# Performer features in a hybrid network: pairs of heads in 32 rows of the array, four chunks of tokens per call

## The chip, the core and the metric

The kernel runs on one core of a Trainium2 chip. A core has a matrix engine (TensorE, "PE" in the profile, with "PEld" for its weight loads), a vector engine (VectorE, "DVE"), a scalar engine for activation functions (ScalarE, "ACT"), a general engine (GpSimd, "POOL"), and a queue for transfers (SyncE, "SP"). They run side by side and wait for each other by semaphores. TensorE reads its operands from the on-chip memory (SBUF) and writes to a second one (PSUM), which has 8 banks of 512 f32 columns on 128 partitions. The metric is device time in microseconds (us), from one launch, as the median of several runs.

## What is computed

The network takes `x` of shape (8, 128, 16, 16), in f32: 8 images of 256 tokens with 128 features. It runs an adder convolution, a Mamba block, an attention with a mixture of experts, a Performer with eight layers, and a spectral layer. The change is in the Performer's attention. Its reference, cut to that:

```python
B, W, D, H, DEP, LAT = (8, 8192, 128, 8, 4, 10)   # H = 8 heads
DH = D // H                                       # 16
M = 44                                            # random features of a head

def softmax_kernel(data, proj, is_query, eps=0.0001):
    dn = data.shape[-1] ** (-0.25)
    ratio = proj.shape[0] ** (-0.5)
    dd = jnp.einsum('bhnd,md->bhnm', data * dn, proj)
    diag = jnp.sum(data * data, axis=-1, keepdims=True) * 0.5 * (dn * dn)
    if is_query:
        mx = jnp.max(dd, axis=-1, keepdims=True)
    else:
        mx = jnp.max(dd, axis=(-1, -2), keepdims=True)
    return ratio * (jnp.exp(dd - diag - mx) + eps)

def attn(t, i):
    q = (t @ Wq[i] + bq[i]).reshape(Bb, N, H, DH).transpose(0, 2, 1, 3)
    ...
    q = apply_rotary(q, sin, cos)
    k = apply_rotary(k, sin, cos)
    qp = softmax_kernel(q, proj[i], True)
    kp = softmax_kernel(k, proj[i], False)
    d_inv = 1.0 / jnp.einsum('bhnm,bhm->bhn', qp, jnp.sum(kp, axis=2))
    ctx = jnp.einsum('bhnm,bhnd->bhmd', kp, v)
    o = jnp.einsum('bhnm,bhmd->bhnd', qp, ctx) * d_inv[..., None]
    ...
    return o @ Wo[i] + bo[i]

for i in range(lo, lo + DEP):
    t = t + attn(layer_norm(t, ln1_g[i], ln1_b[i]), i)
    u = layer_norm(t, ln2_g[i], ln2_b[i])
    t = t + (jax.nn.gelu(u @ W1[i] + b1[i], approximate=False) @ W2[i] + b2[i])
```

`dd` are the features: each head's 16 values of a token against 44 random vectors. The same 44 vectors serve all heads.

## The kernel before

**Tokens and streams.** The activations lie as [128 features, 2048 tokens]. They are cut into 4 blocks of 512 tokens (`BLK`), two images each. In the Performer two *streams* (`_performer_stream`, line 1327) run two blocks each. Each stream has its own pools: `two` and `many` in SBUF, and `psum` with four banks (line 1227), so that the two streams share the eight banks evenly. `bank(S, shape, name)` (line 1263) takes the next of a stream's four banks in turn, and waits until the tile that held it four allocations ago is done with.

**Who goes when.** The streams are Python generators. `interleave` (line 1257) steps both in turn, from yield to yield, and that order of tracing is the order of priority for the scheduler. The scheduler then sorts the instructions of each engine by readiness. Stream 0 starts 16 steps (`HALF_LAYER`) before stream 1. Inside a layer the two blocks of a stream are stepped in turn too (line 1351). A layer of a stream is: a layer norm (`_norms`, 3 steps), the attention of both blocks (`_performer_attention`, line 1402), a second layer norm, the first MLP matmuls with GELU (`p1`, `g3`, lines 1360 to 1365, 4 steps), and the second MLP matmuls (`p2`, line 1370, 2 steps). In the profile both MLP matmuls are called `p`: `p<-u,lw` is the first, `p<-g,lw` the second.

**ACT's tables.** `Tables.use` (line 277) preloads a table of activation functions and orders ACT's instructions around it: everything traced before it comes before it. GELU has its own table. If an Exp or Ln of the other stream stands in a GELU stretch, the build inserts loads around it; in the profile these are ACT_TABLE_LOAD rows.

**The attention of one block,** in the order of its code:

- `rotated` (line 1412): keys and queries by one matmul each (`pa`), bias and rotary angles on DVE (`ro`, `rk`, `rq`), the sum of both parts on POOL (line 1426). Squares for `diag` go through ACT and a matmul (`sq`, `pl`, `dg`).
- *Features of the keys* (lines 1459 to 1471): for each of four chunks of 128 tokens one matmul, `pf` [128 tokens, 8 heads x 44]. The stationary operand is the chunk of `k`, 128 rows (the features of all heads) by 128 tokens. The moving operand `w["f"]` [128, 352] is block-diagonal: the 16 rows of a head hold the 44 vectors in that head's 44 columns, zeros elsewhere. DVE takes the maximum of each head (`mxk`) and subtracts it (`ek`); ACT takes the exponential.
- The maximum over all tokens (lines 1474 to 1486; `m2`, `pm`, `gm`, `dm`, `pg`), the factors that it leaves, and the values `pv`, `vo`.
- *Features of the queries*, function `query(c)`: the same as for keys for chunk `c`, with the maximum of each token and head and its `diag`. Two chunks are done here (lines 1524 to 1527).
- *The context* (lines 1531 to 1556): `pc`, keys' features times values; for each pair of heads and each chunk one matmul with `ek` as stationary operand [128, 88] and 34 moving columns. Then `ks` and `ctx`.
- `turned(c, ex)`: four transposes `px`, one for each pair of heads (88 rows), and one ACT copy to `qp` [88, pair, 512 tokens] (line 1522). The loop of lines 1558 to 1562 turns chunk `c` and computes query chunk `c + 2`.
- `pn` (lines 1565 to 1574): queries' features times context, with 32 output columns for each pair of heads, so that four pairs lie in four groups of columns of the array; then the division (`rd`), the output matmul `po`, and the sum into `H`.

All matmuls are f32. Line 265 is the helper `mm`; most matmuls stand under it and are told apart by their tiles.

Of the kernel before, what the change touches and what calls it, by code (L numbers as in the profile page):

```python
# [10 lines left out]
F32 = mybir.dt.float32  # L11
AF = mybir.ActivationFunctionType
ALU = mybir.AluOpType
AX = mybir.AxisListType
PSUM = bass.MemoryType.PSUM

P = 128
# [3 lines left out]
BLK = 512  # L21
# [14 lines left out]
NH = 8  # L36
DH = 16
M = 44
HM = NH * M
PAIR = 2 * M  # L40
NPAIR = NH // 2
PD = 2 * DH
# [252 lines left out]
def bc(ap, axis, n):  # L295

    a = ap.unsqueeze(axis)
    shape = list(a.shape)
    shape[axis] = n
    return a.to_broadcast(shape)  # L300
# [561 lines left out]
class _Fuse:  # L862
# [23 lines left out]
    def bank(self, shape, name):  # L886
        return self.psum.tile(shape, F32, tag="f", name=name)
# [439 lines left out]
def _performer_stream(S, blocks):  # L1327
# [18 lines left out]
    for i in range(NL):  # L1346
        w = _layer(S, i)
        sums = [two.tile([P, 2], F32, tag=f"us{j}", name="us3") for j in range(2)]
        us = yield from _norms(S, h, S.v(f"ln1_g{i}"), S.v(f"ln1_b{i}"), sums)
        parts = [_performer_attention(S, i, w, h[j], us[j], sums[j], j) for j in range(2)]  # L1350
        while parts:
            parts = [p for p in parts if next(p, None)]
# [49 lines left out]
def _performer_attention(S, i, w, H, u, sums, j):  # L1402
# [6 lines left out]
    nc, two, many = S.nc, S.two, S.many  # L1409
    ident = S.c("ident")  # L1410

    def rotated(name):
        pa = bank(S, [P, 2, L], "pa3")
        S.mm(pa.rearrange("p b l -> p (b l)"), w[name], u)
        bias = S.v(f"b{name}{i}")
        r = two.tile([P, 2, L], F32, tag="r" + name, name="r" + name)
        o = many.tile([P, 2, L], F32, tag="t", name="ro3")
        nc.vector.scalar_tensor_tensor(o, pa, bias, bc(S.c("sin"), 1, 2), ALU.add, ALU.mult)

        sq = many.tile([P, BLK], F32, tag="t", name="sq" + name)  # L1420
        nc.scalar.activation(sq, pa.rearrange("p b l -> p (b l)"), AF.Square, bias=bias)
        nc.vector.scalar_tensor_tensor(r, pa, bias, bc(S.c("cos"), 1, 2), ALU.add, ALU.mult)  # L1422
        o = o.rearrange("p b l -> p (b l)")
        nc.vector.stream_shuffle(o, o, EXCHANGE)
        r = r.rearrange("p b l -> p (b l)")
        nc.gpsimd.tensor_add(r, r, o)  # L1426
        return r, sq

    k, sqk = rotated("k")
    yield True  # L1430
    q, sqq = rotated("q")
# [18 lines left out]
    dg = two.tile([P, 4, 2, NH], F32, tag="dg", name="dg3")  # L1450
# [6 lines left out]


    mx = two.tile([P, 4, NH], F32, tag="mxk", name="mxk")
    ek = two.tile([P, 4, HM], F32, tag="ek", name="ek3")  # L1460
    for c in range(4):
        yield True
        pf = bank(S, [P, HM], "pf3")
        S.mm(pf, k[:, c * P : (c + 1) * P], w["f"])
        f = pf.rearrange("p (h m) -> p h m", m=M)
        nc.vector.tensor_reduce(mx[:, c, :], f, AX.X, ALU.max)
        e = ek[:, c, :]
        nc.vector.tensor_tensor(  # L1468
            e.rearrange("p (h m) -> p h m", m=M), f, bc(mx[:, c, :], 2, M), ALU.subtract
        )  # L1470
        nc.scalar.activation(e, e, AF.Exp, scale=0.5)  # L1471
    yield True

# [29 lines left out]

    qp = two.tile([P, NPAIR, BLK], F32, tag="g", name="qp")[0:PAIR]

    def query(c):
        pf = bank(S, [P, HM], "pq3")
        S.mm(pf, q[:, c * P : (c + 1) * P], w["f"])
        f = pf.rearrange("p (h m) -> p h m", m=M)
        mq = two.tile([P, NH], F32, tag="mq", name="mq")  # L1510
        nc.vector.tensor_reduce(mq, f, AX.X, ALU.max)
        nc.vector.tensor_tensor(mq, mq, dg[:, c, 1, :], ALU.add)
        ex = two.tile([P, HM], F32, tag=f"ex{j}", name="ex")
        nc.vector.tensor_tensor(ex.rearrange("p (h m) -> p h m", m=M), f, bc(mq[:, :], 2, M), ALU.subtract)
        nc.scalar.activation(ex, ex, AF.Exp, scale=0.5)
        return ex

    def turned(c, ex):
        px = bank(S, [PAIR, NPAIR, P], "px3")
        for n in range(NPAIR):  # L1520
            nc.tensor.transpose(px[:, n, :], ex[:, n * PAIR : (n + 1) * PAIR], ident)  # L1521
        nc.scalar.activation(qp[:, :, c * P : (c + 1) * P], px, AF.Identity, bias=S.keps[0:PAIR, :])  # L1522

    ex = []
    for c in range(2):
        yield True
        ex.append(query(c))

    yield True

# [1 line left out]
    for b in range(2):  # L1532
        S.mm(pc[:, b, :, :], ub[:, b, :], wv, start=True, stop=False)
        for n in range(NPAIR):
            for c in (2 * b, 2 * b + 1):
                S.mm(
                    pc[:, b, n, :],
                    ek[:, c, n * PAIR : (n + 1) * PAIR],
                    vo[:, c * NPAIR + n, :],
                    start=False,  # L1540
                    stop=n == NPAIR - 1 and c == 2 * b + 1,
                )
        if b == 0:
            yield True
# [10 lines left out]
        bc(ks[:, :, :], 3, DH),  # L1555
        ALU.mult,
    )
    for c in range(4):
        yield True
        turned(c, ex[c])  # L1560
        if c + 2 < 4:
            ex.append(query(c + 2))

    yield True
    pn = [bank(S, [P, BLK], "pn3") for _ in range(2)]
# [201 lines left out]
```

## Time and profile before

| what | value |
|---|---|
| three runs, median (lowest to highest) | 3185.94 us (3185.02 to 3186.75) |
| the profiled execution's own time | 3185.76 us |
| its span, first to last instruction | 3184.0 us, granted TensorE clock 0.985 |
| PE busy over the span | 2947.6 us (93%), 16686 matmul records |
| DVE busy | 2437.6 us (77%) |
| ACT busy | 2204.9 us (69%) |
| key features: matmul records, weight loads | 256 and 256 (128 matmuls) |
| query features: matmul records, weight loads | 256 and 256 (128 matmuls) |
| context matmuls `pc<-vo,ek` | 1024 records |
| transposes `px` | 512 records |

An engine is busy when one of its instructions runs. A busy TensorE is not TensorE at its peak, because matmuls overlap in the array and their ends are modelled. A group of instructions is written as line, engine, operation, output <- inputs, shape, count, then busy us, mean ns of one, and the idle time before them with what ended it. A timeline line starts with the start in us from the beginning of the span, and the us it covers.

The first two thirds of the span are the adder convolution (to about 1000 us) and the Mamba block (to about 1850 us). The Performer's layers run from about 1960 to 2920 us, and the spectral layer ends the kernel.

### The profile page before, as it was taken

Reading aid. Unit: us, or ns where it says so; the run is one execution under the profiler, and the core shown is the slowest. Engines: PE = TensorE matmul, PEld = TensorE weight load, DVE = VectorE, ACT = ScalarE, POOL = GpSimd, SP = SyncE. Lnnn points to the kernel's source line nnn. Section 1 sums busy time; section 2 is a strip of 40 time slices with the busy share of each in tenths; the row PEclk is TensorE's granted clock in tenths of the full one; section 3 lists DMA queues with packets and bytes.
Section 4 is the critical chain, followed back from the end, with each engine's and each line's share of the span. In section 5 each row is a group of like instructions: output and inputs, shape, how many; then the busy total and the mean of one; then the engine's idle time right before and its main releaser. Section 6 shows DMA issues by size and latency. Waiting matters only on the chain.

```text
span 3184.0 us, 42472 instructions
## 1 busy us (share of the span) xinstructions
PE 2947.6 (93%) x16686; PEld 1299.8 (41%) x16686; DVE 2437.6 (77%) x3419; ACT 2204.9 (69%) x2653; POOL 732.8 (23%) x433
## 2 busy tenths in 40 slices
PE   6999999999997778998997988999999999999999
PEld 2333332333332223333433444555555555555444
DVE  6999999999996999999999257676576577574531
ACT  6999999999995887778776143666667766767111
POOL 3000000000001788778878000010010010010110
PEclk9999999999998999999999998999999999999999
DMA  1000000000001443443443000000000000001100
GB/s 38 1 1 5 1 1 5 1 1 5 1 1 47 166 147 127 146 142 127 151 141 125 17 27 13 1 13 1 13 13 1 13 13 1 13 1 37 53 27 14
DMA packets 39196, 131.47 MB, mean 41 GB/s; under 512 B 7490, under 2 KB 10572, under 8 KB 37588
## 3 DMA queue, kind: packets, MB, share of 16 engines
q1 hardware_dynamic: 38564, 128.02, 11.9%
q8 instruction: 132, 2.16, 0.3%
q10 hardware_dynamic: 432, 0.73, 0.1%
q14 instruction: 68, 0.56, 0.1%
HBM read 125.85 MB, written 1.84 MB: 40 GB/s over the span
## 4 chain that ended last, share of the span: by engine, by line
PE 65%; DVE 22%; ACT 6%; POOL 4%; issue 2%; DMA 1%; DVEq 0%; ACTq 0%; POOLq 0%; SPq 0%
PE o L265 30%; PE p L265 8%; DVE st L839 8%; DVE hc L848 4%; PE g L265 3%; PE pc L265 3%; PE conv L265 3%; PE acc L265 2%; PE pq L265 2%; PE xc L265 2%; PE var L265 2%; POOL dbu L753 2%; PE pv L265 1%; PE pn L265 1%; PE px L1521 1%
## 5 line engine op out<-in xcount | busy, mean ns | idle before, releaser
L265 PE MATMUL o<-d,sel 128*32 128x512 f32 x8800 | 946.4, 592 | 5.5 <-DVE d L432 5.5
L434 ACT ACTIVATE d<-sh,w 128x2048 f32<-128x2048 f32 x460 | 886.3, 1996 | 63.3 <-PE o L265 54.8
L432 DVE TENSOR_SCALAR d<-sh,w 128x2048 f32<-128x2048 f32 x640 | 789.4, 1291 | 47.5 <-PE o L265 39.8
L753 POOL TENSOR_TENSOR dbu<-du,bs 128x1024 f32<-128x1024 f32 x191 | 447.1, 2368 | 1019.4 <-DVE du L727 990.5
L265 PEld LDWEIGHTS o<-d,sel 128*32 128x32 f32 x8800 | 298.2, 110 | 653.0 <-issue 540.9
L839 DVE TENSOR_TENSOR_SCAN st<-da,dbu 128x512 f32<-128x512 f32 x384 | 447.9, 1207 | 13.3 <-POOL dbu L753 11.3
L265 PE MATMUL acc<-hc,cst 128*128 128x512 f32 x768 | 377.3, 616 | 84.8 <-DVE hc L848 84.3
L766 ACT ACTIVATE da<-delta,neg_a 128x510 f32<-128x510 f32 x384 | 256.6, 685 | 81.4 <-DVE st L839 80.4
L265 PEld LDWEIGHTS acc<-hc,cst 128*128 128x128 f32 x768 | 137.1, 192 | 293.4 <-DVE hc L848 173.1
L848 DVE TENSOR_TENSOR hc<-st,pcs 128x1024 f32<-128x1024 f32 x192 | 234.5, 1221 | 25.4 <-ACT tok L894 0.5
L1426 POOL TENSOR_TENSOR rk<-rk,ro 128x512 f32<-128x512 f32 x32 | 40.8, 1275 | 890.3 <-DVE rk L1422 620.5
L758 ACT COPY pcs<-cs 128x512 f32<-128x512 f32 x192 | 112.6, 586 | 79.9 <-DVE hc L848 78.5
L1699 ACT COPY ug<-p 128x512 f32<-128x512 f32 x64 | 37.5, 586 | 177.0 <-PE p L265 177.0
L265 PE MATMUL p<-u,lw 128*128 128x512 f32 x256 | 128.7, 621 | 15.2 <-DVE u L1321 13.3
L265 PE MATMUL conv<-pad,f 128*128 128x512 f32 x288 | 133.8, 598 | 3.2 <-ACT pad L994 2.1
L426 DVE SCALAR_TENSOR_TENSOR d<-sh,w,d 128x2048 f32<-128x2048 f32 x52 | 122.3, 2352 | 1.9
L265 PE MATMUL p<-T,H 128*128 128x512 f32 x256 | 115.6, 602 | 7.3 <-DVE ug L1701 6.3
L1471 ACT ACTIVATE ek<-ek 128x352 f32<-128x352 f32 x128 | 59.8, 492 | 88.0 <-DVE ek L1468 87.8
L1522 ACT ACTIVATE qp<-px,keps 88x512 f32<-88x512 f32 x128 | 84.2, 678 | 51.8 <-PE px L1521 51.2
L265 PE MATMUL p<-g,lw 128*128 128x512 f32 x256 | 114.6, 595 | 0.8 <-ACT g L1363 0.8
L265 PE MATMUL g<-ug,me 128*128 128x512 f32 (+1 forms) x320 | 112.0, 509 | 0.0
L1299 ACT ACTIVATE lsq<-xc 128x512 f32<-128x512 f32 x80 | 47.4, 596 | 76.3 <-PE xc L265 76.2
(322 smaller groups left out, 4064.0 us busy)
## 6 DMA issues: line engine op xcount, KB each, us to landing
bs<-rows SPq DMA_DIRECT2D x96, 512.0 KB, 3.9
cs<-rows SPq DMA_DIRECT2D x96, 512.0 KB, 4.8
m<-in_Mphi SPq DMA_DIRECT2D x8, 1024.0 KB, 4.9
lw<-in_layers SPq DMA_DIRECT2D x8, 948.0 KB, 4.6
f<-in_fuse SPq DMA_DIRECT2D x2, 1152.0 KB, 8.1
T<-in_T SPq DMA_DIRECT2D x1, 2064.0 KB, 8.1
x<-in_x SPq DMA_DIRECT2D x4, 256.0 KB, 6.2
total<-sums SPq DMA_DIRECT2D x16, 64.0 KB, 2.0
```

The source lines that it names most:

```text
L265: self.nc.tensor.matmul(out, lhsT=lhsT, rhs=rhs, start=start, stop=stop)
L426: nc.vector.scalar_tensor_tensor(held, tap(k), w[:, k, f : f + 1], held, ALU.max, ALU.add)
L432: nc.vector.tensor_scalar(d, tap(k), wk, None, ALU.max)
L434: nc.scalar.activation(d, tap(k), AF.Abs, scale=-1.0, bias=wk)
L753: gen.tensor_tensor(dbs[r], got[r // NST]["du"], bc(row("bs", r), 1, 2), ALU.mult)
L758: nc.scalar.copy(pcs[r], row("cs", r))
L766: nc.scalar.activation(das[g % 3][:, :, 1:], d[:, :, 1:], AF.Exp, scale=a)
L839: nc.vector.tensor_tensor_scan(st[:, h, :], da, dbs[r][:, h, :], 0.0, ALU.mult, ALU.add)
L848: nc.vector.tensor_tensor(hc, st, bc(pcs[r][:, :], 1, 2), ALU.mult)
L1299: nc.scalar.activation(sq, xc, AF.Square)
L1471: nc.scalar.activation(e, e, AF.Exp, scale=0.5)
L1522: nc.scalar.activation(qp[:, :, c * P : (c + 1) * P], px, AF.Identity, bias=S.keps[0:PAIR, :])
```

## The change

The block-diagonal product is cut into its pairs of heads. A pair has 32 rows of `k` or `q` and of `w["f"]`, and 88 columns. A new function `features` takes four banks, one for each pair, and runs for each of the four chunks of tokens one matmul for each pair: 16 matmuls with 32 rows, 128 stationary and 88 moving columns. Bank `n` then holds the features of pair `n` for all four chunks, and DVE and ACT go bank by bank (pair by pair) and no longer chunk by chunk. `ek`, `ex` and `qp` follow that layout. The query features now all come after the context matmuls, and the transposes and the copy to `qp` run pair by pair. The yields between chunks are gone: an attention has 9 yields where it had 17.

```diff
-    ek = two.tile([P, 4, HM], F32, tag="ek", name="ek3")
-    for c in range(4):
-        yield True
-        pf = bank(S, [P, HM], "pf3")
-        S.mm(pf, k[:, c * P : (c + 1) * P], w["f"])
-        f = pf.rearrange("p (h m) -> p h m", m=M)
-        nc.vector.tensor_reduce(mx[:, c, :], f, AX.X, ALU.max)
-        e = ek[:, c, :]
-        nc.vector.tensor_tensor(
-            e.rearrange("p (h m) -> p h m", m=M), f, bc(mx[:, c, :], 2, M), ALU.subtract
-        )
+    ek = two.tile([P, NPAIR, 4, PAIR], F32, tag="ek", name="ek3")
+
+    def features(src, name):
+        pf = [bank(S, [P, 4, PAIR], name) for _ in range(NPAIR)]
+        for c in range(4):
+            for n in range(NPAIR):
+                rows = slice(n * PD, (n + 1) * PD)
+                S.mm(pf[n][:, c, :], src[rows, c * P : (c + 1) * P], w["f"][rows, n * PAIR : (n + 1) * PAIR])
+        return [p.rearrange("p c (h m) -> p c h m", m=M) for p in pf]
+
+    yield True
+    for n, f in enumerate(features(k, "pf3")):
+        m = mx[:, :, 2 * n : 2 * n + 2]
+        nc.vector.tensor_reduce(m, f, AX.X, ALU.max)
+        e = ek[:, n]
+        nc.vector.tensor_tensor(e.rearrange("p c (h m) -> p c h m", m=M), f, bc(m, 3, M), ALU.subtract)
         nc.scalar.activation(e, e, AF.Exp, scale=0.5)
     yield True
...
-    def query(c):
-        pf = bank(S, [P, HM], "pq3")
-        S.mm(pf, q[:, c * P : (c + 1) * P], w["f"])
...
+    def query(n, f):
+        mq = two.tile([P, 4, 2], F32, tag="mq", name="mq")
         nc.vector.tensor_reduce(mq, f, AX.X, ALU.max)
...
-    def turned(c, ex):
-        px = bank(S, [PAIR, NPAIR, P], "px3")
-        for n in range(NPAIR):
-            nc.tensor.transpose(px[:, n, :], ex[:, n * PAIR : (n + 1) * PAIR], ident)
-        nc.scalar.activation(qp[:, :, c * P : (c + 1) * P], px, AF.Identity, bias=S.keps[0:PAIR, :])
-
-    ex = []
-    for c in range(2):
-        yield True
-        ex.append(query(c))
+    def turned(n, ex):
+        px = bank(S, [PAIR, BLK], "px3")
+        for c in range(4):
+            nc.tensor.transpose(px[:, c * P : (c + 1) * P], ex[:, c, :], ident)
+        nc.scalar.activation(qp[:, n, :], px, AF.Identity, bias=S.keps[0:PAIR, :])
...
-                    ek[:, c, n * PAIR : (n + 1) * PAIR],
+                    ek[:, n, c, :],
...
-    for c in range(4):
-        yield True
-        turned(c, ex[c])
-        if c + 2 < 4:
-            ex.append(query(c + 2))
+    yield True
+    pf = features(q, "pq3")
+    ex = []
+    for n in range(NPAIR + 1):
+        if n < NPAIR:
+            ex.append(query(n, pf[n]))
+        if n:
+            turned(n - 1, ex[n - 1])
```

More of the change, by code (lines that the diff above doesn't have):

```diff
@@ L1504, in _performer_attention @@
     qp = two.tile([P, NPAIR, BLK], F32, tag="g", name="qp")[0:PAIR]
-    def query(c):
-        pf = bank(S, [P, HM], "pq3")
-        S.mm(pf, q[:, c * P : (c + 1) * P], w["f"])
-        f = pf.rearrange("p (h m) -> p h m", m=M)
-        mq = two.tile([P, NH], F32, tag="mq", name="mq")
+    def query(n, f):
+        mq = two.tile([P, 4, 2], F32, tag="mq", name="mq")
         nc.vector.tensor_reduce(mq, f, AX.X, ALU.max)
-        nc.vector.tensor_tensor(mq, mq, dg[:, c, 1, :], ALU.add)
-        ex = two.tile([P, HM], F32, tag=f"ex{j}", name="ex")
-        nc.vector.tensor_tensor(ex.rearrange("p (h m) -> p h m", m=M), f, bc(mq[:, :], 2, M), ALU.subtract)
+        nc.vector.tensor_tensor(mq, mq, dg[:, :, 1, 2 * n : 2 * n + 2], ALU.add)
+        ex = two.tile([P, 4, PAIR], F32, tag=f"ex{j}", name="ex")
+        nc.vector.tensor_tensor(ex.rearrange("p c (h m) -> p c h m", m=M), f, bc(mq[:, :, :], 3, M), ALU.subtract)
         nc.scalar.activation(ex, ex, AF.Exp, scale=0.5)
         return ex
-    def turned(c, ex):
-        px = bank(S, [PAIR, NPAIR, P], "px3")
-        for n in range(NPAIR):
-            nc.tensor.transpose(px[:, n, :], ex[:, n * PAIR : (n + 1) * PAIR], ident)
-        nc.scalar.activation(qp[:, :, c * P : (c + 1) * P], px, AF.Identity, bias=S.keps[0:PAIR, :])
-    ex = []
-    for c in range(2):
-        yield True
-        ex.append(query(c))
+    def turned(n, ex):
[3 more added lines that the diff above has]
+        nc.scalar.activation(qp[:, n, :], px, AF.Identity, bias=S.keps[0:PAIR, :])
     yield True
```

## The prediction

> **What bounds the kernel now.** I read the page's slices and chain first, then the windows of single layers, the groups by line, the timeline of TensorE, and the chain inside a layer. The changed code runs only in the eight performer layers, from about 1960 to 2920 us of the span. The chain of work that ended last goes mostly through TensorE:
>
> ```profile
> PE 65%; DVE 22%; ACT 6%; POOL 4%; issue 2%; DMA 1%; DVEq 0%; ACTq 0%; POOLq 0%; SPq 0%
> ```
>
> Windows of one layer of both streams (columns: length, then busy time of PE, weight load, DVE, ACT, POOL, and the granted clock) tell the same of this stage:
>
> ```profile
> 2141.00:2260.70 119.70, 113.47 (x634) 65.10 (x634) 78.17 (x207) 78.23 (x127) 10.34 (x9) 0.97 0.03 9
> 2260.70:2380.30 119.60, 113.46 (x634) 65.24 (x634) 78.07 (x206) 78.23 (x127) 10.26 (x9) 0.97 0.03 9
> 2622.60:2739.40 116.80, 110.53 (x634) 63.02 (x634) 78.11 (x206) 78.23 (x127) 10.21 (x9) 1.00 0.03 9
> ```
>
> TensorE works 95% of a layer of about 119 us, DVE and ACT about 65% each. So time taken off TensorE can shorten a layer, as long as no chain through DVE and ACT takes its place. The groups that the change touches (busy us, mean ns; 2000 to 2960 us):
>
> ```profile
> L265 PE MATMUL pq<-lw,rq 128*128 128x352 f32 x248 | 88.0, 460 | 0.0
> L265 PEld LDWEIGHTS pc<-vo,ek 128*88 128x88 f32 x991 | 85.2, 158 | 3.6 <-issue 3.6
> L1511 DVE TENSOR_REDUCE mq<-pq 128x8 f32<-128x352 f32 x124 | 63.6, 518 | 42.0 <-PE pq L265 42.0
> L1514 DVE TENSOR_TENSOR ex<-pq,mq 128x352 f32<-128x352 f32 x124 | 62.6, 519 | 3.7
> L1515 ACT ACT_TABLE_LOAD x22 | 28.2, 1283 | 0.4
> ```
>
> Means of pipelined instructions overlap, so prices come from starts in TensorE's timeline:
>
> ```profile
> 2226.79 1.37 PE L265 MATMUL pc<-vo,ek 128*88 128x34 f32 x16
> 2227.99 0.45 PE L265 MATMUL pc<-lw,ub 128*88 128x136 f32 x2
> ...
> 2342.07 2.53 PE L265 MATMUL pq<-lw,rq 128*128 128x352 f32 x8
> 2344.44 1.88 PE L265 MATMUL p<-u,lw 128*128 128x512 f32 x4
> ...
> 2433.06 1.13 PE L265 MATMUL pa<-u,lw 128*128 128x512 f32 x2
> 2434.12 1.50 PE L265 MATMUL pn<-qp,ctx 88*32 88x256 f32 x24
> 2435.55 1.12 PE L265 MATMUL pa<-u,lw 128*128 128x512 f32 x2
> ```
>
> Four readings. An f32 matmul stands as two records. Eight pq records take 2344.44 - 2342.07 = 2.37 us, 296 ns each, or 0.84 ns per moving column. Sixteen pc records take 1.20 us, 75 ns each: their 34 columns need only 29 ns, so the load of 88 weight columns sets the pace, 0.85 ns per column. The pn records, on four groups of 32 output columns, take 1.43 / 24 = 60 ns each where 256 columns alone need 215: the array runs them about 3.6 at a time. And the two full-array pa records between pn's take 1.06 us where two times 0.43 is due: entering and leaving a tiled mode costs 0.10 us each.
>
> **The change, part by part.** *The feature matmuls.* There are 64 feature calls (8 layers, 4 blocks, keys and queries). Before, a call is 4 matmuls, 2.37 us; 64 of them are 152 us. After, a call is 16 matmuls, 32 records, each loading 128 weight columns into 32 rows and streaming 88 columns. The stream needs 88 x 0.84 = 74 ns, the load 128 x 0.85 = 109; with pc's few ns between, 112 ns a record, set by the load. What no row of before shows is whether loads into different row groups run at once. Bounds: all at once, 8 x 0.112 + 0.20 of mode changes = 1.10 us a call; one after another, 32 x 0.112 + 0.20 = 3.78 us. The nearest row is pn, whose loads and matmuls on four column groups go side by side, so I take "at once".
>
> The built program does not keep the four groups in turn everywhere. Of the 64 calls, 16 matmuls stand together 40 times; in all they stand in 79 stretches, because the scheduler splits calls where banks come free one by one (two groups in turn, then the third alone, then the fourth). Going down that queue, with 224 ns for a matmul on its rows and none starting ahead of the one before it, gives 89 us, and 79 x 0.20 = 16 us of mode changes: 105 us against 152, a gain of 47. One after another: 64 x 32 x 0.112 = 229, plus 16, is 245, a loss of 93.
>
> The Trainium skill, TensorE: Matmul & The Clock Gate, Part 3, gives 3.07 times for four row groups at 512 columns. As an estimate from it, a call would cost 32 x 0.112 / 3.07 + 0.20 = 1.37 us and the gain would be 64; no run here shows row groups, and the built order allows less.
>
> *Banks and waits.* A call now takes four banks at once, all that a stream owns. The second block's call waits, bank by bank, for DVE's subtraction of the first block's. Behind it in TensorE's queue stand the other stream's matmuls, which wait too. DVE's two passes over a bank take 0.86 us (two by 0.43 in the chain), so the fourth bank comes 3.4 us after the first call. Before, the same chunks ran through the same DVE at the same pace, and 15 waits of mxk for pf cost 10.3 us in all. The first result is later by 1.1 - 0.59 = 0.5 us a call. Bounds: nothing (other matmuls stand between) to 3.4 us for each stream and layer, 54 us in all; I take 0.5, the late start alone, 8 us.
>
> The Trainium skill, TensorEngine Tiling (Array Packing), Gotcha 1: PSUM Pressure, speaks against the change: row tiles must write to different banks. The build has just that: four banks a call. If it bit at every call, the upper bound of 54 would be the price.
>
> *The queries.* Before, two of the four query chunks ran ahead of the context matmuls (pc), under them and the other stream's work. Now all of a block's queries come after the context. That moves 2 x (0.43 + 0.16 + 0.43) = 2.0 us of DVE work per block, 4.1 per stream and layer, into the stretch from the context to pn. The cover is the other stream's MLP. The chain of before shows it just there:
>
> ```profile
> 2351.28 2.69 PE pc L265 x34
> ...
> 2356.04 6.87 PE p L265 x16
> 2362.91 0.44 PE px L1521 x4
> ```
>
> Those 6.87 us are the other stream's second MLP matmuls. But an attention has 9 yields now and not 17, a layer 22 steps and not 30, and the streams still start 16 steps apart, so attention of one meets more of the other's attention: in the built queue, between key features and context there are now only the other's var and pa. Uncovered, 4.1 x 16 = 66 us; covered, 0. I take a fifth, 13 us: queries of one stream still have the other's first MLP matmuls beside them.
>
> *What stays.* DVE's and ACT's instructions keep their number and size (352 elements a pass), as do transposes and copies; the qp copy writes one run of 512 and not four of 128, at 0.677 us either way for want of a row that differs. DMAs and POOL's rotary additions are untouched. ACT's table loads fall from 131 to 107 in the build, 24 x 1.283 = 31 us of ACT work. ACT has 40 us a layer to spare, so I take 0; at best 31.
>
> **The sum.** From the profiled execution's 3185.8 us (span 3184.0, 1.8 around it; median of the runs 3185.9): -47 + 8 + 13 = -26, so 3160 us. Its own range goes from 3139 (banks and queries cost nothing) to 3177 (a third of the queries' bound and 16 for banks).
>
> **The rivals.**
> *A, everything is kept:* TensorE's 47 us and half of the table loads come through. For it: 95% busy. Against it: DVE steps stand in the layer's chain. 3185.8 - 47 - 16 = 3123 us. Chance 0.15.
> *B, row groups load one after another:* place, the weight loads of the feature calls; price 93 us on an engine that is 95% busy, decided from 66 ns a record on (64 x 32 x 0.066 + 16 = 151, what the calls cost before). For it: pc shows that loads, not streams, pace small matmuls, and no row shows two row groups. Against it: column groups do go at once. 3185.8 + 93 - 15 of the table loads = 3264 us. Chance 0.2.
> *C, the streams' chains take over:* the loads go at once, but the banks (54) and the uncovered queries (half of 66) cost more than 47 saves: 3185.8 - 47 + 87 = 3226 us. It decides once more than 47 us of the two bounds' 120 come through. For it: the new phase of the streams; against it: DVE and ACT are a third idle. Chance 0.22.
> *D, no change:* gain and waits cancel within 6 us: 3186. Chance 0.06.
>
> **How the numbers follow.** The forecast, 3160, has 0.37. This kernel's measurement can't tell less than 0.2% (6.4 us) from no change. Faster: 0.37 + 0.15 = 0.52; same 0.06; slower 0.2 + 0.22 = 0.42. The range, 3110 to 3268, reaches from A to B; beyond it I leave the tails of both, under 2 in 10. The forecast's own is 3139 to 3177.
>
> **What would show it.** The loads: starts of four pf records a few ns apart, and a call of 16 in about 1.1 us, show "at once"; 3.8 us show B. The banks: DVE waiting for pf, and weight loads of pf waiting for ek, beyond the 10 us of before, show C; so does TensorE's busy share of a layer falling below 90% with a layer still at 119 us or more. The queries: ACT's qp and DVE's mq on the chain between pc and pn, without p beside them. Table loads: 24 fewer. The prediction is wrong if a layer does not come down to about 116 us.

## The result, and the profile after

The changed kernel takes 3367.48 us (median of 4 runs, 3366.05 to 3369.57) against 3186.35 us for the kernel before on the same chip: 1.0569 times as long, 95% interval 1.0552 to 1.0585. The prediction said 3160, with a range that ended at 3268.

The page of the changed kernel, the row of the granted TensorE clock in 40 slices (tenths of full speed), and the shares of the chain that ended last by engine:

```profile
PEclk9999999999999999999999888878788787878999
...
PE 67%; DVE 20%; ACT 6%; POOL 4%; issue 2%; DMA 1%; DVEq 0%; ACTq 0%; POOLq 0%
```

The chain's shares hardly differ from before. The clock row does: it stands at 7 or 8 from the 23rd slice to the 37th, 1852 to 3115 us, which are all but two short ends the eight performer layers (from about 1940 us on). The same row of the kernel before has two slices at 8 and the rest at 9:

```profile
PEclk9999999999998999999999998999999999999999
```

Two layers of the changed kernel in the view by windows (length, then busy us of PE, weight load, DVE, ACT, POOL, the granted clock, DMA share, GB/s):

```profile
2192.10:2332.20 140.10, 127.13 (x831) 76.25 (x827) 77.55 (x205) 75.72 (x125) 10.18 (x8) 0.81 0.02 8
2624.40:2765.50 141.10, 128.11 (x831) 76.54 (x827) 78.26 (x207) 76.12 (x125) 11.43 (x9) 0.81 0.02 8
```

A layer takes 140 to 141 us and not the 119 of before. TensorE is busy for 127 of them, which looks like more work; but at a clock of 0.81 these are 127.13 x 0.81 = 103 us of work at full speed, against 113.46 x 0.97 = 110 before. So TensorE does have less to do, it does it slowly, and it also waits longer: 13 us a layer without a matmul, against 6.

To keep these three things apart, I split the whole performer stage (from its first rotation matmul `pa` to its last transposition) by the trace: the time in which a matmul runs, cut at each change of the granted clock. *Work* is that time multiplied by the granted clock; *lost to the clock* is the rest of it; *idle* is the time without a matmul.

| performer stage, us | length | work at full clock | lost to the clock | idle |
|---|---|---|---|---|
| before | 1006 | 926 | 22 | 58 |
| after | 1184 | 878 | 186 | 121 |
| difference | +178 | -48 | +164 | +63 |

(In the last 62 us of the stage, 32 in the kernel before, some first matmuls of the spectral layer run too; counted from 1935 us to the end of the kernel, where that does not matter, work differs by -43 and the other two by the same +164 and +63.)

TensorE's timeline in the changed kernel shows the lost time (start, us covered, line, output <- inputs, shapes, records, idle before):

```profile
2475.11 1.40 PE L265 MATMUL pf<-lw,rk 32*128 32x88 f32 x31
...
2507.31 0.64 PE L1523 MATMUL px<-cst,ex 128*88 128x128 f32 x4 [0.80 <-ACT ex L1517]
2509.11 0.64 PE L1523 MATMUL px<-cst,ex 128*88 128x128 f32 x4 [1.16 <-ACT ex L1517]
...
2518.52 1.08 PE L1523 MATMUL px<-cst,ex 128*88 128x128 f32 x4
2519.53 2.10 PE L265 MATMUL pf<-lw,rk 32*128 32x88 f32 x12
2521.57 1.08 PE L1523 MATMUL px<-cst,ex 128*88 128x128 f32 x4
2522.58 1.15 PE L265 MATMUL pf<-lw,rk 32*128 32x88 f32 x4
2523.66 1.08 PE L1523 MATMUL px<-cst,ex 128*88 128x128 f32 x4
2524.67 7.06 PE L265 MATMUL pn<-qp,ctx 88*32 88x256 f32 x64
```

A feature call of 32 records takes 1.14 us at best where the clock is full, against the 3.78 worked out for groups one after another: the four row groups do run at once (other calls of this kernel take up to 2.9 us). The clock is halved from 2510.4 to 2537.7 us, and there everything takes about double: four transposes 1.08 us in place of 0.64, 64 `pn` records 7.06 us where 60 ns each (the row of before) gives 3.8. What stands there is the query stretch of one stream (`px`, `pn`) and, between, the key features of the other (`pf`). No MLP matmul of 512 columns is among them. Ahead of it `px` waits for `ex`, because the chain from query features to transposes (maximum, sum, difference, exponential) now runs behind the context. The view of waits of weight loads (us in total, times, longest) over the performer stage, before and then after:

```profile
PEld px L1521 <- ACT ex L1515: 3.0, 9, 1.1
```

```profile
PEld px L1523 <- ACT ex L1517: 62.6, 67, 2.2
...
PEld pf L265 <- DVE ek L1475: 2.7, 7, 0.4
```

The wait of the transposes' weight loads for `ex` rises from 3.0 to 62.6 us. That is not all idle time of TensorE, because other matmuls can run while a weight load waits. TensorE's own wait at the same place is

```profile
PE px L1523 <- ACT ex L1517: 38.8, 36, 2.0
```

where it was 0.9 before: some 38 of the 63 us. The next largest rise is the wait of `pm` for `m`, the keys' maximum, from 0.3 to 18.7 us. The wait of `pf` for the banks is 2.7 us: no price there.

### The profile page after: what moved, and what is told of

Read it like the earlier page. It is cut to its first block, busy times and chain, and to the rows that moved or that the text cites. A ratio compares the mean times of both kernels' runs of the same rounds, so it can differ in the third digit from the quotient of the medians.

```text
span 3367.8 us, 45566 instructions
## 1 busy us (share of the span) xinstructions
PE 3070.2 (91%) x18222; PEld 1396.4 (41%) x18222; DVE 2434.8 (72%) x3419; ACT 2182.7 (65%) x2629; POOL 733.0 (22%) x433
## 4 chain that ended last, share of the span: by engine, by line
PE 67%; DVE 20%; ACT 6%; POOL 4%; issue 2%; DMA 1%; DVEq 0%; ACTq 0%; POOLq 0%
PE o L265 28%; PE p L265 8%; DVE st L839 8%; DVE hc L848 4%; PE g L265 3%; PE pn L265 3%; PE px L1523 3%; PE pc L265 3%; PE xc L265 2%; PE conv L265 2%; PE pa L265 2%; PE acc L265 2%; PE pf L265 2%; PE po L265 2%; PE pq L265 1%
## 5 line engine op out<-in xcount | busy, mean ns | idle before, releaser
L1523 PE MATMUL px<-cst,ex 128*88 128x128 f32 x512 | 103.8, 364 | 38.9 <-ACT ex L1517 38.8
L1517 ACT ACTIVATE ex<-ex 128x352 f32<-128x352 f32 x128 | 58.8, 490 | 94.7 <-DVE ex L1516 93.8
L1580 DVE TENSOR_TENSOR rd<-pn,rd 128x512 f32<-128x512 f32 x32 | 21.7, 690 | 130.7 <-ACT rd L1578 82.4
```

Of the source, the lines that this page charges most:

```text
L1523: nc.tensor.transpose(px[:, c * P : (c + 1) * P], ex[:, c, :], ident)
```

## The experiments

Three theories came out of this reading. T1: the changed schedule leaves stretches in which the array has too little to do, and the clock falls for that. T2: matmuls in 32-row tiles do not count as work for the clock, however many there are. T4: banks and the moved queries lengthen a chain, and the clock is a companion. T3, the streams' phase, and T5, the query chain whatever the phase, were split off from T1 after the first runs. The table after the last experiment has every kernel's stage.

### Full-array features in the same places

```
-                rows = slice(n * PD, (n + 1) * PD)
-                S.mm(pf[n][:, c, :], src[rows, c * P : (c + 1) * P], w["f"][rows, n * PAIR : (n + 1) * PAIR])
+                S.mm(pf[n][:, c, :], src[:, c * P : (c + 1) * P], w["f"][:, n * PAIR : (n + 1) * PAIR])
```

> The changed kernel with the same banks, order and layout, but each feature matmul on all 128 rows (the projection is block diagonal, so the values stay the same): 64 calls x 32 records x 0.112 us = 3.6 us a call in place of 1.1, 160 us more TensorE work at full clock. T1 (the clock falls because this schedule leaves stretches with too little for the array to do): the array is filled in these stretches, mean granted clock 0.96 or more, total 3270 to 3340, faster than the changed kernel (3367) in spite of more work. T2 (row-tiled matmuls do not count for the clock): the same here. T4 (no matter of the clock: banks and the queries' chain): 3367 plus up to 160, 3450 to 3527, clock still near 0.93.

Measured: 3363.78 us, clock 0.97, against 3184.32 before on this chip. Stage: work 993, lost to the clock 67, idle 121. The kernel has 115 us more of TensorE work than the changed one and loses 119 us less to the clock; idle is the same. The time is neither theory's number, but the split is T1's (or T2's): fill the array in these stretches and the clock comes back, about as much as was filled in. T4, which kept the clock at 0.93, falls.

### Keys alone, queries alone

The first has the changed `pf` part and the query code of before, the second the reverse.

> Only the keys' half of the change; queries as before (two chunks ahead of the context, two behind). T1 with the query stretch as its place: clock 0.97 or more, 3140 to 3180. T2 (row tiling itself starves the gate): half of the loss, about 3275, clock 0.955. T4 with the four banks as its price: 3230 or more at a clock of 0.98.

> Only the queries' half of the change; keys as before. T1 with the query stretch as its place: nearly the whole loss, 3320 to 3370, clock 0.93 to 0.94. T2: half, about 3275. T4 (moved queries on the chain): 3230 to 3300 at a clock of 0.98.

Measured: keys alone 3222.59 us (ratio 1.012, 1.0103 to 1.0137), idle +16 and clock +36 against before; queries alone 3244.70 (1.0188, 1.0173 to 1.0203), idle +49 and clock +23. My place for T1, the query stretch, was wrong: each half costs about 40 to 60 us. No theory's number holds for the keys (T4 asked for 3230 or more); for the queries T4's does (3230 to 3300 at a clock of 0.98, measured 0.976). The idle terms add up (16 + 49 = 65; both together 63). The clock terms do not: 36 + 23 = 59, together 164. In both, layers have fewer steps than before (27 and 25 of 30), with the second stream still 16 behind.

### What the clock follows

The first probe, TensorE alone, stretch by stretch:

```
        full(60); row(800, 88); full(30); full88(200); full(30); turn(360)
        full(30); col(400); full(30); small(320); full(30); row(240, 512); full(30)
```

> Not the model: TensorE alone with stretches of one kind of f32 matmul each, some 30 to 45 us at full clock, with full-array 512-column matmuls between (the output is not the reference's). T2: the granted clock falls to 0.50 in the 32-row, 88-column stretch within about 7 us of its start, and it takes 90 us and not 45. T1: it stays at 1.00 there, as in the full-array stretches, and falls at most where few columns are streamed (34-column context-like matmuls, transposes).

The windows of its stretches (length, busy us of PE, weight load, DVE, POOL, granted clock), in this order: 32-row tiles with 88 columns, full array with 88, transposes, 32-column tiles with 256, context-like matmuls (88 weight columns, 34 moving), 32-row tiles with 512:

```profile
59.50:104.30 44.80, 44.80 (x1601) 44.76 (x1600) 0.00 (x0) 0.00 (x0) 1.00 0.02 4
130.20:174.80 44.60, 44.60 (x401) 44.59 (x400) 0.00 (x0) 0.00 (x0) 1.00 0.00 1
200.60:239.90 39.30, 39.30 (x361) 39.27 (x360) 0.00 (x0) 0.00 (x0) 1.00 0.01 1
265.80:309.00 43.20, 43.20 (x801) 25.87 (x800) 0.00 (x0) 0.00 (x0) 1.00 0.01 2
334.90:423.30 88.40, 88.40 (x641) 88.36 (x639) 0.00 (x0) 0.00 (x0) 0.53 0.00 1
450.80:502.50 51.70, 51.70 (x481) 24.49 (x480) 0.00 (x0) 0.00 (x0) 1.00 0.00 1
```

T2 falls: row tiles, four at a time, keep the clock at 1.00, as transposes and column tiles do. Only the 34-column matmuls lose it, though TensorE is busy in every ns of that stretch. And 800 row-tiled matmuls take 44.8 us where 200 of the full array take 44.6: four at once, exactly.

The second probe varies the columns of the context-like matmul alone.

> Not the model: TensorE alone, stretches of 320 matmuls with 88 weight columns and 72, 60, 52, 44, 40 and 34 moving columns (48 us each at full clock, set by the weight loads), full-array 512-column matmuls between. Columns need 0.84 ns each of the 75 ns of a record, shares 0.81, 0.67, 0.58, 0.49, 0.45, 0.38. If the gate follows the streamed share: the wide ones keep 1.00, the narrow ones fall to 0.50 after some 12 us, with one boundary between. If it follows the queue's being busy, the 34-column stretch alone fell by accident.

Windows of 72, 60, 52, 44, 40 and 34 columns; the first four are all like the 40-column one, shown with the 34-column one:

```profile
396.60:446.70 50.10, 50.10 (x641) 50.06 (x640) 0.00 (x0) 0.00 (x0) 1.00 0.01 2
481.10:570.30 89.20, 89.20 (x641) 89.17 (x640) 0.00 (x0) 0.00 (x0) 0.53 0.00 1
```

One record takes 50.1 / 640 = 78 ns in all but the last, set by its weight load. At 0.84 ns a column, 40 columns stream for 0.43 of that and 34 for 0.36 or 0.37. The boundary lies between: in the probe the clock follows the share of time in which columns move through the array, not whether an instruction runs (the section on the hardware checks this inside the model). The context matmuls of this kernel are below it by themselves; they need other matmuls beside them, before the change and after.

### One more matmul in the wait

```
         px = bank(S, [PAIR, BLK], "px3")
+        S.mm(px, w["f"][:, 0:PAIR], u)
         for c in range(4):
```

> The changed kernel with one more 512-column full-array matmul ahead of each pair's four query transposes, into the bank that they then overwrite (128 of them, 0.86 us each, 110 us of TensorE work at full clock, values unchanged). If the lowered clock is a cause and not a companion: clock loss falls from 186 to below 90, and the total is 3270 to 3380 in spite of the added work, most of which stands in waits. If it is a companion: 3367 + 110, some 3480.

Measured: 3359.60 us. Work 989 (111 more), lost to the clock 77 (108 less), idle 113 (8 less); the wait of `px` for `ex` falls to 12.9 us. Doing 111 us of useless work costs nothing, as was expected if the lowered clock is a cause and not a companion. But full-array features had cancelled as closely (+115, -119), so another limit close below, in the chain through DVE and ACT, would look alike. The chain that ended last tells more: in the stage of the changed kernel it runs 354 us through TensorE at half clock, in the kernel before 43, so the lowered clock does stand on the chain. What the time would be with the clock back and nothing added, at this distance of the streams, no run shows.

### Queries ahead of the context

```
     yield True
+    ex = [query(n, f) for n, f in enumerate(features(q, "pq3"))]
+    yield True
 
     pc = bank(S, [PAIR, 2, NPAIR, PD + 2], "pc3")
...
-    pf = features(q, "pq3")
```

> The changed kernel with all of a block's query features, maxima, differences and exponentials ahead of the context matmuls (in tiles that the rotated keys and queries leave free); only transposes and copies stay behind. T5: idle falls to 60 to 80 and the clock loss to 60 or less, total 3150 to 3220. T3: the phase is nearly kept (steps 16 of 23), idle about 110 and clock loss over 120, total 3300 or more.

Measured: 3239.01 us. Idle falls to 51, less than before's 58, and `px` waits for `ex` hardly at all. So at this distance of the streams the idle time comes with the moved queries, as T5 says. (The edit also makes a layer 24 steps long, so the distance is not quite the same share.) The clock loss stays at 98 us, as neither says, and the time is in neither's range. TensorE's timeline of this kernel shows a place of it:

```profile
2503.17 2.46 PE L265 MATMUL pc<-vo,ek 128*88 128x34 f32 x16
2505.44 0.73 PE L265 MATMUL pc<-lw,ub 128*88 128x136 f32 x2
2505.97 2.47 PE L265 MATMUL pc<-vo,ek 128*88 128x34 f32 x16
```

The context matmuls stand in one piece of 11 us here with nothing between, at 2.46 us for 16 where 1.20 was the price at full clock: the probe's 34-column stretch inside the model.

### The streams' phase

One constant, `HALF_LAYER`, says how many steps the second stream runs behind the first. It is 16 in both kernels, but a layer has 30 steps before and 22 after. First the changed kernel with half a layer, and the kernel before with the changed one's share:

```
-HALF_LAYER = 16
+HALF_LAYER = 11
```

> The changed kernel with the second stream 11 steps behind the first in place of 16: half of the new layer of 22 steps. So far, over the performer stage: the changed kernel's TensorE work at full clock is 48 us less than before, its idle time 63 us more, its loss to the lowered clock 164 us more. T3 (the streams' phase puts one's attention beside the other's, so that nothing fills the waits): idle 60 to 80, clock loss 20 to 60, total 3140 to 3200. T5 (the query chain behind the context leaves the stretch empty whatever the other stream does): idle about 120, total 3320 or more.

> The kernel before with its second stream 22 of 30 steps behind (the same share of a layer as 16 of 22), nothing else. T3: idle and clock loss rise by most of 63 and 164, total 3300 to 3400. T5: 3180 to 3230.

Measured: the changed kernel at 11 takes 3218.37 us (4 runs, 3197.53 to 3219.67), 149 less than at 16. Idle is 77, clock loss 45, as T3 asked, though in the fastest of the four runs; the median misses T3's 3140 to 3200 by 18 us. T5, which kept idle at about 120 whatever the phase, falls as a full account. The kernel before at 22 of 30 takes 3185.75: no change, T3 missed there. Then more phases, each with the number it had to meet:

> The changed kernel with the second stream 20 of 22 steps behind: nearly in step with the first. T3 (the price is one stream's attention beside the other's): the worst phase of all, idle over 121, clock loss about 186 or more, total 3350 to 3500. If 16 is bad by some accident of the built order and not by the phase: anywhere from 3190 to 3370.

> The changed kernel, 13 of 22 steps. T3: between 11 (3218) and 16 (3367), nearer to 11: 3210 to 3270, idle 75 to 95, clock loss 45 to 100.

> The changed kernel, 9 of 22 steps: the other side of 11. T3: the same as 13, 3190 to 3270, since the roles of the streams only change; lower than 11 if the first MLP matmuls cover the queries better than the second ones.

> The changed kernel, 8 of 22 steps. T3: past the middle, where the first MLP matmuls lie beside the queries: 3165 to 3200, idle 60 to 70, clock loss 25 to 45.

> The changed kernel, 7 of 22 steps. T3: 3170 to 3230; if the best phase lies below 9 it is faster than the kernel before, 3150 to 3175.

> The changed kernel, 10 of 22 steps, between 9 (3191) and 11 (3218). If the phase decides: 3175 to 3220, idle 65 to 80, clock loss 35 to 50. If details of the built order decide, as the step from 9 to 8 (3191 to 3353) suggests: it may be as high as 3300.

> The kernel before with its streams nearly in step (27 of 30, the share of 20 of 22, which cost the changed kernel 3446). If any kernel of this kind pays for attention beside attention: 3280 or more, idle over 90, clock loss over 90. If only the changed one does (calls of 16 short matmuls and queries in one piece leave more to be covered): 3180 to 3220.

And two combinations of a phase of half a layer with one part of the change (a layer with the queries ahead has 24 steps, not the 23 of the expectation, so 12 is just half):

> Queries ahead of the context (as in the run with 3239) and half of its 23 steps as phase. If the two causes add (idle was 51 with queries ahead, clock loss 45 with the phase): stage work 885 to 910, idle 50 to 60, clock loss 25 to 50, total 3140 to 3200, at or below the kernel before. If they are one cause: no better than phase alone, 3200 to 3220.

> Keys alone, half of its 27 steps as phase (13 in place of 16, which gave 3222 with work 910, idle 74, clock loss 58). If the phase was its price too: idle 60 to 70, clock loss 25 to 45, total 3165 to 3205, at best faster than the kernel before. If the four banks at once are the price whatever the phase: 3215 or more.

All of them, the stage by its profiled execution beside the median (at 9, 10 and 11 the profiled execution was 10, 11 and 21 us faster than the median, so their losses stand rather low):

| kernel | steps behind | median us | work | lost to the clock | idle |
|---|---|---|---|---|---|
| before | 16 of 30 | 3184 to 3186 | 926 | 22 | 58 |
| before | 22 of 30 | 3185.8 | 934 | 17 | 61 |
| before | 27 of 30 | 3259.3 | 927 | 56 | 99 |
| after | 7 of 22 | 3318.8 | 879 | 125 | 121 |
| after | 8 of 22 | 3352.9 | 881 | 164 | 117 |
| after | 9 of 22 | 3191.5 | 883 | 40 | 66 |
| after | 10 of 22 | 3211.7 | 885 | 43 | 73 |
| after | 11 of 22 | 3218.4 | 885 | 45 | 77 |
| after | 13 of 22 | 3322.6 | 892 | 133 | 104 |
| after (as changed) | 16 of 22 | 3367.5 | 878 | 186 | 121 |
| after | 20 of 22 | 3445.9 | 903 | 267 | 97 |
| full-array features | 16 of 22 | 3363.8 | 993 | 67 | 121 |
| fill in the wait | 16 of 22 | 3359.6 | 989 | 77 | 113 |
| queries ahead | 16 of 24 | 3239.0 | 910 | 98 | 51 |
| queries ahead | 12 of 24 | 3242.7 | 909 | 72 | 71 |
| keys alone | 16 of 27 | 3222.6 | 910 | 58 | 74 |
| keys alone | 13 of 27 | 3232.9 | 909 | 65 | 65 |
| queries alone | 16 of 25 | 3244.7 | 908 | 44 | 108 |

Work is the same in every phase of the changed kernel to within some 25 us; the time moves by 254 us, with the clock and the idle time. Nearly in step (20) is the worst, as T3 asked, though its idle time is 97 and not over 121; 9 to 11 are good, with 9 and 10 inside the numbers expected of them. The kernel before pays for a bad phase too, but 75 us (27 of 30, between the two numbers that were offered for it), where the changed one pays up to 254. But the curve is not the smooth one that T3 drew: from 9 to 8 it jumps by 161 us, 7 and 8 miss their expectations by 89 and 153 us, 13 is at 3323 where 3210 to 3270 was expected, and 9 and 13, which are mirror images in a layer of 22 steps, differ by 131. Nor is half a layer a cure for the two combinations: queries ahead stays at 3243, and keys alone gets 10 us worse, inside the range that was set for the four banks as its price. The trace does not bear the banks out: `pf` waits for `ek` 3 us at most in both runs of keys alone. TensorE waits more at other places there (at 16 for `g` ahead of the second MLP matmuls, 27 us against 3; at 13 for the keys' maximum, `pg` for `dm` 27 and `pm` for `m` 16). The phase decides for the changed kernel; why the jumps lie where they lie is in the order that each phase's build gives, and stays open.

TensorE's timeline at 9 shows what a good phase looks like, in the stretch that answers to the one shown of 16:

```profile
2516.07 1.18 PE L265 MATMUL pf<-lw,rk 32*128 32x88 f32 x16
2517.19 1.12 PE L265 MATMUL p<-u,lw 128*128 128x512 f32 x2
...
2536.36 1.14 PE L265 MATMUL pq<-lw,rq 32*128 32x88 f32 x32
2537.43 3.70 PE L265 MATMUL p<-g,lw 128*128 128x512 f32 x8
2540.97 1.04 PE L1523 MATMUL px<-cst,ex 128*88 128x128 f32 x8
2541.84 1.88 PE L265 MATMUL p<-g,lw 128*128 128x512 f32 x4
2543.56 1.04 PE L1523 MATMUL px<-cst,ex 128*88 128x128 f32 x8
...
2552.80 3.66 PE L265 MATMUL pn<-qp,ctx 88*32 88x256 f32 x64
```

MLP matmuls of the other stream (`p<-u,lw`, `p<-g,lw`) stand between row tiles and transposes; they fill part of the wait for `ex` (TensorE itself waits 23.6 us there in place of 38.8, and its weight loads 47.4 in place of 62.6), and `pn` takes 3.66 us where it took 7.06. A layer there, by windows:

```profile
2182.70:2298.70 116.00, 108.90 (x827) 64.24 (x826) 78.97 (x206) 69.70 (x121) 10.23 (x8) 0.99 0.03 9
```

This is the layer that the prediction had: 116 us at a clock of 0.99. Against the kernel before, the version at 9 is still level (1.0013, interval 0.9997 to 1.0029). Its profiled execution (3181.5) has a stage 17 us shorter (work -44, clock +19, idle +8) and gives most of that back at the end: before, the two streams end so far apart that the spectral layer's matmuls start 32 us before the stage is over, at 9 only 8 us before. No version that was run beats the kernel before.

## Why the prediction was wrong, point by point

**The feature matmuls: right.** Predicted -47 us of TensorE work, measured -48 in the stage (-43 to the end). A call of 32 records that nothing splits takes 1.14 us at full clock, 1.10 as worked out; rival B, row groups one after another, is refuted by the timeline and by the probe (800 in 44.8 us).

**Banks: right in being small.** 8 us was charged, with a bound of 54. The wait of `pf` for DVE's `ek` is 2.7 us in the changed kernel, so the four banks at once cost about nothing by themselves. Keys alone did have 16 us more idle time; its largest rise is a wait for `g` in the MLP, and why it rose is open.

**The queries: the mechanism right, the size wrong.** I charged a fifth of 66 us, 13, on the argument that the other stream's MLP covers the chain. Idle time rose by 63, but only some 38 of that is TensorE standing before `px` for `ex`, three times the 13; another 18 is the keys' chain of maxima (`pm` for `m`), for which the sum had no term. With the queries ahead of the context, the wait for `ex` and the added idle time are gone (51). The text named what would undo the cover, "a layer 22 steps and not 30, and the streams still start 16 steps apart", and priced it at a fifth.

**The clock: the term that was missing, and the step that failed.** The sum had work and waits, all at the clock of before, 0.97 to 1.00, and put a lowered clock at nothing. TensorE's busy time lost 186 us to it in place of 22. That is +164 us, nine tenths of the 181; the work saved and the idle time added nearly cancel. Without it the sum, with the idle time at its measured 63 and the banks at nothing, is 3185.8 - 48 + 63 = 3201. Rival C had a right place (queries and the streams' new phase), but at 3226 it is 141 us short, for want of the same term. The profile of before did hold the warning: TensorE was at 0.97 and not 1.00 in two of the three layer windows that the prediction shows; the clock fell twice in each of these two, and ten times in the stage.

**What turned the one into the other.** The change takes the 352-column feature matmuls (0.84 ns a column, streaming all the time) out of just those stretches that also hold context matmuls (streaming 0.36 of the time) and waits. Filling them again, with full-array features or with useless work, returns 108 to 119 us of clock; both put in 111 to 115 us, more than twice what the change had saved there. And it shortens the layer to 22 steps, so that at 16 the other stream's MLP is elsewhere; at 9 to 11 the same work loses only 40 to 45 us to the clock.

**Table loads and what stays: right.** ACT's records fall by 24 (2653 to 2629) and nothing in the time can be put down to it.

**The signs named in advance.** "The prediction is wrong if a layer does not come down to about 116 us": it rose to 140, and comes down to 116 at a phase of 9. "TensorE's busy share of a layer falling below 90%": 127.13 of 140.10 is 91%, a sign that failed, because a slow clock makes an engine look busy. Busy share has to be read with the clock beside it.

## What to carry to other kernels

Multiply a busy share by the granted clock before you call it work, and ask of each stretch, not of the whole, whether matmul columns still stream for at least about 0.4 of the time once the change has made its matmuls shorter; work that is saved there can be paid back as clock. When an edit changes the number of steps of one of two interleaved streams, the constant that sets their phase is part of the edit: try the phases before judging it. A context matmul with 34 columns takes as long as one with 40 (its weight load sets the pace), and 40 held the clock in the probe; padding it inside the model wasn't tried.

## What the runs showed of the hardware

**The clock falls on a busy engine.** In the probes the fall came 6.1 and 5.2 us after the 34-column stretch began, and full speed came back 2.8 and 4.6 us after it ended. The trace's clock only has the values 1.0 and 0.5, in pieces of about 3.41 us or multiples of it. The Trainium skill, TensorE: Matmul & The Clock Gate, Part 1, gives this window as 3413 ns, which agrees; but its rule for staying fast, no idle gaps over some 3.4 us, does not cover the case here: TensorE had no gap at all in those 89 us and ran at half speed.

**The share that decides, inside the model.** For each piece of 3.41 us in the traces of the 18 model kernels, from 1900 us on, add up the columns of all matmul records at 0.84 ns each, every record weighted by the share of the 128 rows that it uses (and for tiles of 32 columns by a further quarter), and divide by 3.41 us. In 6825 of 6918 pieces (98.7%) the next piece had full clock just where this share was above 0.37; a limit on the mere share of time in which any matmul runs does no better than 88.7%. At half clock the share cannot exceed 0.5, so by this count a kernel that has lost the clock gets it back only when columns stream for about three quarters of the time.

**Transposes and tiles count.** 360 transposes in a row held the clock at 1.00 for 39.3 us. The same page, Part 4, says that full clock does not engage for transposes; for these f32 ones the measurement decides: once reached, it holds.

**Runs near the boundary scatter.** The kernel before repeats within 0.2% (3182.85 to 3186.75 us in 15 runs). The changed kernel at 10 ran from 3184.34 to 3224.51 us in ten runs, 1.3%, with a clock of 0.978 in the fastest and 0.970 in the slowest; at 9 from 3176.95 to 3197.22. A schedule that only just keeps its clock does not keep it in each run alike; the reason was not tested.
